# Cross-attention over 32 batches: output adds ahead of a transposition, and the sum of the attention output kept in PSUM

## The chip, the cores and the metric

The kernel runs on one core of a Trainium2 chip. The metric is the device time of one launch in microseconds; the time before is the median of three runs.

Engines are named as in the profile: PE is TensorE (PEld its weight loads), DVE is VectorE, ACT is ScalarE, POOL is GpSimd, SP is SyncE, which here only issues DMAs.

## The reference, cut to what matters

The inputs are `x` (32, 512, 640) and a context (32, 77, 1024), all in float32. The context's first 77 rows are the text keys, and there are only 77, so the object, other and image-prompt parts of the reference are empty and add nothing. What is left:

```
q = heads(x @ to_q_w)                  # 20 heads of 32
k = heads(ctx @ to_k_w); v = heads(ctx @ to_v_w)
p = softmax(q @ k.T / sqrt(32))        # over 77 keys
out = merge(p @ v) @ to_out_w + to_out_b + x
```

## The kernel before, in words

**Precision.** Every float32 operand of a matrix product is split into a high part, rounded to the fast float32 format of PE, and a low part, the rest. A product is then three matmuls: high by high, high by low, low by high. So each operand costs one cast on ACT (the high part) and one subtraction on DVE or POOL (the low part).

**Stages.** The first part of the program (about 300 us) makes keys and values for all batches and leaves them in DRAM. Then come 160 *slots*: slot n is batch b = n // 5 and a group of four heads j = n % 5. `slot` (line 661) writes out by hand, in program order, what each engine's queue holds; there is no scheduler behind it (`manual_schedule`), and every engine works its own queue in order. Semaphores between engines follow from which tiles the instructions touch.

**One slot.** On PE it holds, in this order: the scores of the first 128 queries (`scores(n, 0)`, three matmuls, line 453); six matmuls of the next slot's query projection (`queries`, line 434, tile `pq`); scores 1; nine more `pq` matmuls; scores 2; a piece of the output projection (`piece`, line 604, matmuls of line 589 into tile `po`); the product of probabilities and values (`values`, six matmuls of line 545 into tile `pa`); scores 3; a second `piece`.

On DVE a slot holds the row maxima of each score tile (line 461, `nm`); the low part of the probabilities (line 524, `pp`); the reciprocal of the sums (481); the low part of the attention output (571, `at`); the transposition of the probabilities (493, `z`); the low part of the next queries (104, `qt`); two adds that form the attention output (558); the adds that close output tiles (618, `xr`); and in some slots the transposition of the next batch's `x` (255).

ACT does the exponentials (471) and the casts (`qt` 103, `pp` 517 and 523, `at` 566, `xt` 262) and copies half of `pa` out of PSUM (556). POOL normalizes the probabilities (486), makes the last low part (531) and adds the bias to the residual (582).

**A lag.** The probabilities of slot n go through a transposition and through DRAM (`transpose_p`, `load_p`), and come back three slots later: in slot n the `values` are those of slot n - 3. The output projection of batch b - 1 starts when its five head groups are there, at j = 2 of batch b, in ten pieces over five slots (`STEPS`, `CUTS`, `PIECES`).

**The fourth slot, j = 3.** Its first piece (piece 2, six matmuls) multiplies the fifth head group into the two halves of the first 128 output rows and closes both. Its second piece (piece 3, 18 matmuls) opens the next output tiles. There are only two `po` buffers, so piece 3 can start only when the adds of line 618, called by `finish`, have read the two closed tiles. Before the change these adds stand on DVE's queue behind the `z` transposition and the `qt` subtraction of the slot.

**The sum of the attention output.** `values` leaves four partial results in `pa`, a PSUM tile of two banks with a single buffer. `sum_a` copies the upper 64 partitions to an SBUF tile `aw` on ACT and adds the halves on DVE into `aw`, also in SBUF. `high_a` and `low_a`, which run early in the next slot, make the parts of `at` from `aw`:

```
nc.vector.tensor_tensor(aw[64 * p : 64 * p + 64, 0], pa[:64, p], aw[:64, p], ALU.add)   # sum_a
nc.scalar.copy(at[:, 0, :], aws[n][:, 0])                                               # high_a
nc.vector.tensor_tensor(at[:, 1, :], aws.pop(n)[:, 0], at[:, 0, :].bitcast(F32), ...)   # low_a
```

**The end.** `end` (line 763) runs the last three `take` calls (values, sum, high part, low part one after the other) among what is left of the output projection, and uses `pa`'s two banks for the last two output tiles (`begin(6, ...)` and `begin(7, ...)`).

Of the kernel before, what the change touches and what calls it, by code (L numbers as in the profile page):

```python
# [8 lines left out]
F32 = mybir.dt.float32  # L9
FPR = mybir.dt.float32r  # L10
AF = mybir.ActivationFunctionType
ALU = mybir.AluOpType
# [11 lines left out]
P = 128  # L24
# [27 lines left out]
def kernel(  # L52
# [25 lines left out]
    nc = tc.nc  # L78
    B, S, C = x.shape
# [307 lines left out]
    psv = tc.alloc_tile_pool(name="psv", bufs=3, space=PSUM, side="right", reuse_waits="tile")  # L387
    late = []

    raws, pps, ats, pds, sms, pqs, pas, aws, xrs, pos = ({} for _ in range(10))  # L390

    bias = main.tile([P, C], F32, name="bias")
    nc.sync.dma_start(bias, bo.unsqueeze(0).to_broadcast([P, C]))
# [53 lines left out]
    def scores(n, t):  # L447
        b, j = divmod(n, NC_)
        g = GROUP_OF[j]
        qt, kb = qts[n % 2], kbs[g]  # L450
        sc = ps.tile([P, S], F32, tag="sc", name="sc", bufs=3)
        for m, (a, c) in enumerate(PAIRS):
            nc.tensor.matmul(  # L453
                sc[:, :KCOLS],
                qt[:, a, t * P : (t + 1) * P],
                kb[:, j - GROUPS[g][0], c],
                start=(m == 0),
                stop=(m == 2),
            )
        nm = main.tile([P, HPC], F32, tag="nm", name="nm", bufs=3)  # L460
        nc.vector.tensor_reduce(  # L461
            nm, sc[:, :KCOLS].rearrange("p (h k) -> p h k", k=NKEY), AX.X, ALU.max, negate=True
        )
        return sc, nm
# [14 lines left out]
    def sums(n):  # L479
        rs = main.tile([P, NQ * HPC], F32, tag="rs", name="rs", bufs=2)  # L480
        nc.vector.reciprocal(rs, sms.pop(n))  # L481
        return rs
# [30 lines left out]
    def cast_p(n):  # L513

        raw = raws[n]
        pp = late[0].tile([P, 5, S], FPR, tag="pp", name="pp", bufs=1)
        nc.scalar.copy(pp[:, 0:2, :], raw[:, 0:2, :])  # L517
        pps[n] = pp

    def rest_p(n):  # L520

        raw, pp = raws[n], pps[n]
        nc.scalar.copy(pp[:64, 4, :], raw[:64, 2, :])  # L523
        nc.vector.tensor_tensor(  # L524
            pp[:, 2:4, :], raw[:, 0:2, :], pp[:, 0:2, :].bitcast(F32), ALU.subtract
        )
# [24 lines left out]
            )  # L551

    def sum_a(n):
        pa = pas.pop(n)
        aw = late[0].tile([P, 2, S], F32, tag="aw", name="aw", bufs=1)
        nc.scalar.copy(aw[:64], pa[64:])  # L556
        for p in range(2):
            nc.vector.tensor_tensor(aw[64 * p : 64 * p + 64, 0], pa[:64, p], aw[:64, p], ALU.add)  # L558
        aws[n] = aw

    def high_a(n):
        if n >= N - NC_ + 1:
            at = xpool[0].tile([P, 2, S], FPR, tag="xt", name="at", bufs=7)
        else:
            at = late[0].tile([P, 2, S], FPR, tag="at", name="at", bufs=8)
        nc.scalar.copy(at[:, 0, :], aws[n][:, 0])  # L566
        ats[n] = at

    def low_a(n):
        at = ats[n]  # L570
        nc.vector.tensor_tensor(  # L571
            at[:, 1, :], aws.pop(n)[:, 0], at[:, 0, :].bitcast(F32), ALU.subtract
        )

    def load_residual(b, t, xr=None):
# [8 lines left out]
    def output_bank(b, t, h):  # L584
        pos[b, t, h] = late[1].tile([P, S], F32, tag="po", name="po", bufs=2)

    def project(b, t, h, j):
        for m, (a, c) in enumerate(PAIRS):
            nc.tensor.matmul(  # L589
                pos[b, t, h][:, :HALF],  # L590
                ats[b * NC_ + j][:, a, t * P : (t + 1) * P],
                wos[0][:, j, c, h * HALF : (h + 1) * HALF],
                start=(j == 0 and m == 0),
                stop=(j == NC_ - 1 and m == 2),
            )
# [8 lines left out]
    def piece(b, i):  # L604
        for t, h, j in STEPS[CUTS[i] : CUTS[i + 1]]:
            if j == 0:
                output_bank(b, t, h)
            project(b, t, h, j)
            if j == NC_ - 1:
                closed.append((b, t, h))  # L610

    def finish():

        while closed:
            b, t, h = closed.pop(0)
            xr = xrs[b, t]
            cols = slice(h * HALF, (h + 1) * HALF)
            nc.vector.tensor_tensor(  # L618
                xr[:, cols], pos.pop((b, t, h))[:, :HALF], xr[:, cols], ALU.add
            )  # L620
            if (b, t) == (B - 1, NQ - 1):
                nc.sync.dma_start(out[b, t * P : (t + 1) * P, cols], xr[:, cols])
            elif h == 1:
                nc.sync.dma_start(out[b, t * P : (t + 1) * P, :], xr)
# [23 lines left out]
    def refill(b, j, part):  # L648

        heads = range(2 * part, 2 * part + 2)  # L650
        segments = SEGMENTS[4 * part : 4 * part + 4]
        if j == 0:
            load_keys(b, 1, heads)
        elif j == 1:
            load_values(b, 0, segments)
        elif j == 2 and b + 1 < B:
            load_keys(b + 1, 0, heads)
        elif j == 3:
            load_values(b, 1, segments)

    def slot(n, beside=()):
        b, j = divmod(n, NC_)
        ahead, more = n + 1 < N, b + 1 < B
        back, first = PIECES[j]
        bo_, has_out = b - back, b >= back
        xsplits = SPLIT_X.get(j, ((), ())) if more and n > LATE else ((), ())
        turns = TRANSPOSE_X.get(j, ((), (), ())) if more and b else ((), (), ())
        if b == 1 and j < 2:
            turns = (((), (), ()), ((0, 1), (2,), ()))[j]
        taken = takes.get(n)  # L670

        filling = taken is not None and not has_out
        if not filling:
            refill(b, j, 0)
        if taken is not None:
            cast_p(taken)
        if n - 1 in takes:
            high_a(takes[n - 1])
        s = scores(n, 0)
        if taken is not None:  # L680
            rest_p(taken)
        rs = sums(n - 1) if n else None
        if taken is not None:
            last_p(taken)
        if n:
            normalize(n - 1, rs)
        if n - 1 in takes:
            low_a(takes[n - 1])
        exps(n, 0, *s)
        if ahead:  # L690
            queries(n + 1, 0, 2)
        s = scores(n, 1)
        if n - LAG + 1 in pds and n > LATE:
            load_p(n - LAG + 1)
        if filling:
            refill(b, j, 0)
        if n == NC_:
            load_x(b + 1, (2, 3))
        for k in WO.get(n, ()):
            nc.sync.dma_start(wos[0][:, k].bitcast(F32), wo_dram[:, k].bitcast(F32))  # L700
        refill(b, j, 1)
        finish()
        if j == 4 and b and b + 2 < B:
            load_x(b + 2, (0, 1))
        if j in RESIDUAL and b >= RESIDUAL[j][0]:
            load_residual(b - RESIDUAL[j][0], RESIDUAL[j][1])
        if j in BIAS and b >= BIAS[j][0]:
            add_bias(b - BIAS[j][0], BIAS[j][1])
        exps(n, 1, *s)
        for i in turns[0]:  # L710
            transpose_x(b + 1, i)
        if ahead:
            queries(n + 1, 2, NC_)
        s = scores(n, 2)
        if not ahead:
            exps(n, 2, *s)
            piece(bo_, first)
            s = scores(n, 3)
        if n and has_out:
            transpose_p(n - 1)  # L720
        if ahead:
            split_q(n + 1)
            exps(n, 2, *s)
        if n and not has_out:
            transpose_p(n - 1)
        if j == 4 and b + 2 < B:
            load_x(b + 2, (0, 1) if not b else (2, 3))
        for c in xsplits[0]:
            split_x(b + 1, c)
        if not ahead:  # L730
            exps(n, 3, *s)
            finish()
            piece(bo_, first + 1)
            take(taken)
            return
        if has_out:
            piece(bo_, first)
        else:
            s = scores(n, 3)
        if taken is not None:  # L740
            values(taken)
        if len(beside) > 0:
            context_values(LAST, beside[0], psv)
        if j == 3:
            finish()
        if has_out:
            s = scores(n, 3)
        finish()
        for i in turns[1]:
            transpose_x(b + 1, i)  # L750
        if taken is not None:
            sum_a(taken)
        for c in xsplits[1]:
            split_x(b + 1, c)
        exps(n, 3, *s)
        if len(beside) > 1:
            context_values(LAST, beside[1], psv)
        if has_out:
            piece(bo_, first + 1)
        for i in turns[2]:  # L760
            transpose_x(b + 1, i)
# [96 lines left out]
    for n in range(LATE, N):  # L858
        slot(n)
# [41 lines left out]
```

## Time and profile before

| | |
|---|---|
| median of 3 runs | 2065.09 us (2062.93 to 2071.85) |
| the profiled execution | 2066.77 us, span 2065.0 us |
| PE | 1956.2 us busy, 95% of the span |
| PEld | 1737.1 us, 84% |
| DVE | 1581.4 us, 77% |
| ACT | 1540.4 us, 75% |
| POOL | 1057.4 us, 51% |
| mean granted clock of PE | 0.975 |
| HBM traffic | 208 GB/s over the span |

Matmuls are pipelined and their ends are modelled, so PE's busy time is not time at its peak. The shares are means over the first part, in which DVE and ACT work at some 40%, and the slots, in which they work at over 80%. The order of work repeats every five slots, once for each batch, so the timeline of one batch stands for nearly all.

### The profile page before, as it was taken

The numbers are of one execution on the slowest core, as the hardware profiler recorded it, in microseconds if no ns is written. First come the engines' busy times: TensorE is split into PE (matmuls) and PEld (weight loads), VectorE is DVE, ScalarE is ACT, GpSimd is POOL, SyncE is SP. The second block draws the span as 40 slices with busy tenths as digits, with TensorE's granted clock in tenths as the row PEclk, the third lists the DMA queues.
The fourth block names the chain that finished last, engine by engine and source line by source line (L and its number), as shares of the span: only waits on it lengthen the run. The fifth ranks groups of instructions, "written<-read, shape, count | busy, mean of one in ns | idle before, by whom it ended". The sixth has DMA issues, their size and how long they took to land.

```text
span 2065.0 us, 36489 instructions
## 1 busy us (share of the span) xinstructions
PE 1956.2 (95%) x10332; PEld 1737.1 (84%) x10332; DVE 1581.4 (77%) x2334; ACT 1540.4 (75%) x6210; POOL 1057.4 (51%) x648
## 2 busy tenths in 40 slices
PE   9999997999999999999999999999999999999997
PEld 7787886888888888888888888888888888888886
DVE  4444447888888888888888888888888888888884
ACT  3232248888888888888888888888888888888882
POOL 1000125555665565565555555555665565556543
PEclk9999998999999999999999999999999999999999
DMA  9878787888888888888888888888888888888874
GB/s 184 203 178 233 180 200 206 233 207 219 219 206 212 223 213 208 214 214 213 210 219 214 214 220 211 214 215 210 222 204 213 223 213 212 212 214 213 213 191 134
DMA packets 568281, 431.29 MB, mean 209 GB/s; under 512 B 195344, under 2 KB 477072, under 8 KB 568080
## 3 DMA queue, kind: packets, MB, share of 16 engines
q1 hardware_dynamic: 564848, 417.65, 80.4%
q0 software_dynamic: 3136, 11.14, 1.5%
q8 instruction: 84, 1.38, 0.3%
q14 instruction: 117, 0.96, 0.1%
q10 hardware_dynamic: 96, 0.16, 0.0%
HBM read 247.17 MB, written 181.64 MB: 208 GB/s over the span
## 4 chain that ended last, share of the span: by engine, by line
PE 40%; ACT 16%; issue 15%; DVE 13%; POOL 11%; DMA 3%; SPq 1%; POOLq 0%; DVEq 0%; ACTq 0%
PE po L589 15%; PE pq L434 11%; POOL pn L486 8%; ACT pn L471 6%; PE sc L453 5%; PE pa L545 5%; ACT aw L556 3%; POOL pp L531 3%; PE pv L191 2%; PE pk L191 2%; DVE at L571 2%; DVE aw L558 2%; DMA pd<-z 2%; DVE qt L104 2%; ACT pp L523 2%
## 5 line engine op out<-in xcount | busy, mean ns | idle before, releaser
L471 ACT ACTIVATE pn<-sc,nm 128x77 f32<-128x77 f32 x2560 | 800.6, 333 | 221.5 <-DVE nm L461 217.4
L589 PE MATMUL po<-wo_s,at 128*128 128x320 f32 x3840 | 667.5, 323 | 81.6 <-DVE xr L618 65.3
L589 PEld LDWEIGHTS po<-wo_s,at 128*128 128x128 f32 x3840 | 606.8, 198 | 106.7 <-DVE xr L618 85.1
L434 PE MATMUL pq<-xt,wq_s 128*128 128x512 f32 x2400 | 607.3, 394 | 0.0
L531 POOL TENSOR_TENSOR pp<-raw,pp 64x512 fp32r<-64x512 f32 x160 | 217.5, 1360 | 662.4 <-ACT pp L523 589.4
L471 ACT ACTIVATION_READ_ACCUMULATOR pn<-sc,nm 128x1 f32 x2560 | 542.9, 212 | 0.0
L434 PEld LDWEIGHTS pq<-xt,wq_s 128*128 128x128 f32 x2400 | 438.1, 189 | 75.6
L486 POOL TENSOR_TENSOR pn<-pn,rs 128x1232 f32<-128x1232 f32 x160 | 412.8, 2580 | 59.7 <-DVE rs L481 48.9
L453 PE MATMUL sc<-kb,qt 128*128 128x308 f32 x1920 | 379.6, 306 | 11.8 <-ACT pn L471 8.5
L461 DVE TENSOR_REDUCE nm<-sc 128x4 f32<-128x308 f32 x640 | 296.0, 467 | 111.8 <-PE sc L453 107.3
L453 PEld LDWEIGHTS sc<-kb,qt 128*128 128x128 f32 x1920 | 326.6, 189 | 57.5 <-ACT pn L471 9.5
L493 DVE STREAM_TRANSPOSE z<-pn 128x1280 f32<-128x1280 f32 x160 | 241.8, 1511 | 115.6 <-POOL pn L486 100.4
L545 PE MATMUL pa<-pp,vb 128*128 128x512 f32 x960 | 253.3, 399 | 1.6 <-DVE pp L524 0.8
L524 DVE TENSOR_TENSOR pp<-raw,pp 128x1024 fp32r<-128x1024 f32 x160 | 208.1, 1301 | 45.6 <-ACT pp L517 44.4
L558 DVE TENSOR_TENSOR aw<-pa,aw 64x512 f32<-64x512 f32 x320 | 216.0, 675 | 33.9 <-ACT aw L556 27.9
L571 DVE TENSOR_TENSOR at<-aw,at 128x512 fp32r<-128x512 f32 x160 | 236.0, 1475 | 3.0 <-ACT at L566 3.0
L263 POOL TENSOR_TENSOR xt<-xs,xt 128x512 fp32r<-128x512 f32 x160 | 203.2, 1290 | 65.1 <-ACT xt L262 34.7
L556 ACT COPY aw<-pa 64x1024 f32<-64x1024 f32 x160 | 161.7, 1011 | 72.4 <-PE pa L545 70.9
L545 PEld LDWEIGHTS pa<-pp,vb 128*128 128x128 f32 x960 | 175.3, 189 | 32.2 <-DVE pp L524 1.1
L582 POOL TENSOR_TENSOR xr<-xr,bias 128x640 f32<-128x640 f32 x128 | 200.0, 1564 | 0.1
L517 ACT CAST pp<-raw 128x1024 fp32r<-128x1024 f32 x160 | 168.9, 1055 | 4.4 <-DMA raw<-pd 4.4
L191 PE MATMUL pk<-ct,wk_s 128*128 128x512 f32 (+1 forms) x600 | 139.3, 392 | 8.4 <-ACT ct L103 5.9
(42 smaller groups left out, 1364.7 us busy)
## 6 DMA issues: line engine op xcount, KB each, us to landing
pd<-z SPq DMA_DIRECT2D x640, 160.0 KB, 3.1
raw<-pd SPq DMA_DIRECT2D x160, 512.0 KB, 3.9
xs<-in_x_dram SPq DMA_DIRECT2D x128, 320.0 KB, 5.7
xr<-in_x_dram SPq DMA_DIRECT2D x128, 320.0 KB, 3.7
out_dram<-xr SPq DMA_DIRECT2D x127, 320.0 KB, 3.9
raw<-pd SPq DMA_DIRECT2D x160, 128.0 KB, 4.1
v_dram<-vs SPq DMA_DIRECT2D x80, 192.0 KB, 4.0
k_dram<-ks POOLq DMA_DIRECT2D x20, 512.0 KB, 3.3
```

Of the source, the lines that this page charges most:

```text
L434: nc.tensor.matmul(pqs[n], wq_s[:, k, a, j * P : (j + 1) * P], xts[b, k][:, c, :], start=(k == 0 and m == 0), stop=(k == NC_ - 1 and m == 2),)
L453: nc.tensor.matmul(sc[:, :KCOLS], qt[:, a, t * P : (t + 1) * P], kb[:, j - GROUPS[g][0], c], start=(m == 0), stop=(m == 2),)
L461: nc.vector.tensor_reduce(nm, sc[:, :KCOLS].rearrange("p (h k) -> p h k", k=NKEY), AX.X, ALU.max, negate=True)
L471: nc.scalar.activation(pnb[n % 2][:, at, :NKEY], sc[:, i * NKEY : (i + 1) * NKEY], AF.Exp, bias=nm[:, i : i + 1], accum_out=sms[n][:, at : ...
L486: nc.gpsimd.tensor_tensor(pf, pf, rs.unsqueeze(2).to_broadcast([P, NQ * HPC, NKEY]), ALU.mult)
L493: nc.vector.transpose(z.rearrange("p b t j -> p t b j"), pn.rearrange("p (t h) k -> p t (h k)", t=NQ).rearrange("p t (b i) -> p t b i", i=Q),)
L531: nc.gpsimd.tensor_tensor(pp[64:, 4, :], raw[:64, 2, :], pp[:64, 4, :].bitcast(F32), ALU.subtract)
L545: nc.tensor.matmul(pas[n][:, p, :], vb[:, p, t, :], pp[:, c, :], start=(c == p), stop=(t == 1),)
L556: nc.scalar.copy(aw[:64], pa[64:])
L558: nc.vector.tensor_tensor(aw[64 * p : 64 * p + 64, 0], pa[:64, p], aw[:64, p], ALU.add)
L571: nc.vector.tensor_tensor(at[:, 1, :], aws.pop(n)[:, 0], at[:, 0, :].bitcast(F32), ALU.subtract)
L589: nc.tensor.matmul(pos[b, t, h][:, :HALF], ats[b * NC_ + j][:, a, t * P : (t + 1) * P], wos[0][:, j, c, h * HALF : (h + 1) * HALF], start= ...
```

## The change

There are two edits.

In slot j = 3 the first piece and the call of `finish` that closes its two outputs move ahead of `transpose_p` and `split_q`. On PE nothing moves: the matmuls stand in the same order as before. On DVE the two adds of line 618 now stand ahead of the `z` transposition and the `qt` subtraction. On SP's queue the store of the finished output rows stands ahead of the four stores of `z`. ACT and POOL keep their order.

In `sum_a` the two adds of DVE write their result back into `pa` in PSUM, and `aw` keeps only the copied half (64 partitions). `high_a` and `low_a` read `pa`. In the built program the second of the two adds now also waits on a semaphore of DVE itself, which it did not before. `pa` is released by `low_a`, in the next slot, and no longer by the adds.

```diff
     def sum_a(n):
-        pa = pas.pop(n)
-        aw = late[0].tile([P, 2, S], F32, tag="aw", name="aw", bufs=1)
-        nc.scalar.copy(aw[:64], pa[64:])
+        pa = pas[n]
+        aw = late[0].tile([64, 2, S], F32, tag="aw", name="aw", bufs=1)
+        nc.scalar.copy(aw, pa[64:])
         for p in range(2):
-            nc.vector.tensor_tensor(aw[64 * p : 64 * p + 64, 0], pa[:64, p], aw[:64, p], ALU.add)
-        aws[n] = aw
+            nc.vector.tensor_tensor(pa[64 * p : 64 * p + 64, 0], pa[:64, p], aw[:, p], ALU.add)
 
     def high_a(n):
...
-        nc.scalar.copy(at[:, 0, :], aws[n][:, 0])
+        nc.scalar.copy(at[:, 0, :], pas[n][:, 0])
         ats[n] = at
 
     def low_a(n):
         at = ats[n]
         nc.vector.tensor_tensor(
-            at[:, 1, :], aws.pop(n)[:, 0], at[:, 0, :].bitcast(F32), ALU.subtract
+            at[:, 1, :], pas.pop(n)[:, 0], at[:, 0, :].bitcast(F32), ALU.subtract
         )
...
             piece(bo_, first)
             s = scores(n, 3)
+        if j == 3 and has_out:
+            piece(bo_, first)
+            finish()
         if n and has_out:
             transpose_p(n - 1)
         if ahead:
...
         if has_out:
-            piece(bo_, first)
+            if j != 3:
+                piece(bo_, first)
         else:
             s = scores(n, 3)
         if taken is not None:
             values(taken)
         if len(beside) > 0:
             context_values(LAST, beside[0], psv)
-        if j == 3:
-            finish()
         if has_out:
             s = scores(n, 3)
         finish()
```

## The prediction

> **What bounds the kernel now.** I read the page first. PE is the bound by its busy share (95%); DVE and ACT are at 77 and 75% of a span whose first 15% uses them less than half, so in the slots they are near 84% (the page's slices, and a mean of 167 to 168 us busy in the 200 us windows from 400 to 2000 us). Next I asked which wait PE still has:
>
> ```profile
> PE 1956.2 (95%) x10332; PEld 1737.1 (84%) x10332; DVE 1581.4 (77%) x2334; ACT 1540.4 (75%) x6210; POOL 1057.4 (51%) x648
> L589 PE MATMUL po<-wo_s,at 128*128 128x320 f32 x3840 | 667.5, 323 | 81.6 <-DVE xr L618 65.3
> PE po L589 <- DVE xr L618: 65.3, 33, 3.4
> PE po L589 <- DVE at L571: 8.6, 30, 0.9
> ```
>
> The group's row says that 81.6 us of PE's 109 us of idle time stand before one kind of matmul; the list of waits says whom it waited for: 33 times the closing adds, 2 us each, and 30 times the low part of `at`. One batch has one of each, so I looked at the fourth slot in the timeline (start, duration, engine, instruction, idle time before):
>
> ```profile
> 1018.93 1.67 DVE L571 TENSOR_TENSOR at<-aw,at 128x512 fp32r<-128x512 f32 x1
> 1019.52 0.59 PE L453 MATMUL sc<-kb,qt 128*128 128x308 f32 x3
> 1020.13 2.60 POOL L486 TENSOR_TENSOR pn<-pn,rs 128x1232 f32<-128x1232 f32 x1
> 1020.52 0.85 DVE L461 TENSOR_REDUCE nm<-sc 128x4 f32<-128x308 f32 x2
> 1020.65 0.85 PE L589 MATMUL po<-wo_s,at 128*128 128x320 f32 x4 [0.25 <-DVE at L571]
> 1021.34 1.55 PE L545 MATMUL pa<-pp,vb 128*128 128x512 f32 x6
> 1022.74 0.58 PE L453 MATMUL sc<-kb,qt 128*128 128x308 f32 x3
> 1022.77 1.51 DVE L493 STREAM_TRANSPOSE z<-pn 128x1280 f32<-128x1280 f32 x1 [1.39 <-POOL pn L486]
> 1024.20 0.65 DVE L104 TENSOR_TENSOR qt<-pq,qt 128x512 fp32r<-128x512 f32 x1
> 1024.78 0.87 DVE L618 TENSOR_TENSOR xr<-po,xr 128x320 f32<-128x320 f32 x2
> 1025.31 2.91 PE L589 MATMUL po<-wo_s,at 128*128 128x320 f32 x18 [1.99 <-DVE xr L618]
> ```
>
> The two `po` tiles are complete at about 1021.4, but DVE first idles 1.39 us for POOL, transposes, makes `qt`, and only then closes them. PE stands still from 1023.3 to 1025.31. Everything else on PE in this batch follows without a gap.
>
> The stall costs a second time. In the next batch the same 18 matmuls take 4.42 us instead of 2.91, and the windows' row shows the granted clock there:
>
> ```profile
> 1078.87 4.42 PE L589 MATMUL po<-wo_s,at 128*128 128x320 f32 x18 [1.99 <-DVE xr L618]
> 1078.80:1082.20 3.40, 3.33 (x15) 3.33 (x16) 2.17 (x5) 3.37 (x11) 3.17 (x3) 0.64 0.95 201
> ```
>
> The clock is 0.64 over this stretch, and 0.50 in each full microsecond of its middle. It was 1.00 in the same stretch of the batch before. Of the 31 such stalls in the timeline 20 are followed by the long form, 11 by the short, and from the first of them to the last the granted clock is halved nowhere else.
>
> **The change part by part.** *The adds ahead of the transposition.* They need the six matmuls of piece 2 (end about 1021.4, or 0.4 earlier without the wait for `at`) and two row maxima ahead of them. Two adds take 0.87 us, so they end by about 1022.3, before PE reaches the 18 matmuls at 1023.3. Of the waits 30 are of about 1.98 us (65.3 less the last three, 1.47, 1.16 and 3.35, leaves 59.3) and one, in the last batch, is of 1.47; these 31 go: 60.8 us. The 1.16 and the 3.35 lie elsewhere in the last batch and stay.
>
> What is moved back: DVE's `z` and `qt` now stand behind a wait for PE and 0.87 us of adds. The cover is that DVE idles 1.39 us there anyway, for POOL's normalization, which ends at 1022.73. `z` so starts when it did, `qt` ends at about 1024.85 as now, and the fourth row maximum comes 0.87 us earlier. Who waits for `qt` is scores 0 of the next slot; PE, no longer stopped, gets there at 1023.3 + 18 x 0.146 = 1025.9. So the next thing that could be late has about 1 us to spare; without that cover each late microsecond would stop PE in every batch. On SP the store of the output rows now stands ahead of the four `z` stores; it issues in 0.72 us and waits for adds that end before `z` does: nothing.
>
> *The slow clock.* If the 2 us stall goes, I take the half clock with it: 20 x (4.45 - 2.91) = 30.8 us. The row is my reason: no half clock follows the stalls of 0.25 us, nor the one of 1.47 us. The Trainium skill ("TensorE: Matmul & The Clock Gate", Part 1) speaks against this: it lets the clock fall after an idle window of about 3.4 us, and the idle time here is 2 us. By that rule the half clock would have another cause and stay, and the sum would be 30.8 us higher; the measured coincidence, 20 of 20, decides for me.
>
> *The sum in PSUM.* `low_a` has two SBUF inputs and takes 1.62 us in the median where POOL works beside it, but 0.69 at the end, where POOL is idle. Read from PSUM, its shape is that of the `qt` subtraction, 0.65 us. That is 160 x (1.475 - 0.654) = 131 us of DVE's time. On the path lies little of it: the 30 waits of PE for `at` go, 8.6 us; bounds are 0 and 12 (the four matmuls start 0.4 us late by their own rhythm). `high_a` reads PSUM at 0.60 instead of 0.63: nothing on the path.
>
> No row of this trace writes PSUM from DVE. The nearest is the add itself, 0.68 us with a PSUM input and SBUF output. In its new form I bound it by 0.64 us, its fastest now, and by 1.36, if a write to PSUM cost as much again, and take 0.68, since only the output moves; the new wait of the second add on the first is bounded by 0 and by a whole add, and I take 0.05, near the hop from ACT's copy to DVE's add in the tail (0.03). Both lie on DVE, which has just been given 0.95 us a slot, so nothing on the path.
>
> `pa` is held until `low_a`. In the fourth slot `low_a` ends 0.74 us before PE writes `pa` again, in the other four 1.8 us or more (1009.77 against 1011.61 in the third); with the shorter `low_a` these grow by 0.95. Nothing in the slots. In the tail it costs: the 12 matmuls of `begin(6)`, at 2053.81, wait for the adds, which end at 2053.66; now they wait for the low part, which ends at 2055.09. That is 1.4 us, once.
>
> **Sum.** 60.8 + 30.8 + 8.6 - 1.4 = 98.8 us. The profiled execution took 2066.77 us, 1.7 above the median; 2066.8 - 98.8 = 1968.0, or 1966 against the median. I predict 1967. A cross-check: batches are now 54.59 us apart on average (1583.13 us between 30 stalls); 53.57 - 1.98 - 0.3 = 51.3 us would be left, and ACT, 45.5 us busy in a batch, and DVE, 45.8 less 4, still fit into that.
>
> **Rivals.** *The half clock stays*, for the reason given or because a shorter gap still sets it off: 2066.8 - 68 = 1999 us. For it: the gap's limit is not known better than between 1.47 and 2 us. Chance 0.12.
>
> *The stall moves.* ACT and DVE, which PE now outruns, become late elsewhere: `qt` in the fourth slot, or the `xr` adds in the fifth and first, where the 12 matmuls at 1046.44 already take 2.31 us instead of 1.92. Against: ACT idles 1.2 us in each of these slots because of the slow `low_a`, which ends. If half of the stall returned, the half clock mostly gone, 2066.8 - 30 - 25 = 2012 us; if all of it returned, with the clock, about 2058, which is no change. Chance 0.12, of which 0.03 for the last.
>
> *Slower: `pa` is released too late.* `low_a` stands on DVE behind `pp`, which waits for ACT's cast. If it ended later than PE's next `values` by d, PE would stop d in all 155 slots. It decides against the change from d = 0.7 (155 x 0.7 = 108 us, more than the gain); that needs `low_a` to end 1.4 us later than now in the fourth slot and 2.5 in the others, while its own time shrinks. The dear end of the adds' price, 2 x 0.68 less the 0.95 saved, is 0.4 of these. At d = 0.8 the time is 2066.8 - 99 + 124 = 2092 us. Chance 0.04.
>
> *It does not do what it says*: only if the adds could not run early, for instance for the bias; but POOL adds it a slot ahead (line 582, ended by 1013.5). No chance of its own.
>
> **How the numbers follow.** Forecast 0.72, half clock stays 0.12, stall moves 0.12, slower 0.04. The forecast's own range: below, the 0.39 us still hidden in the first slot goes too (31 x 0.39 = 12, 1955); above, half of the half clocks stay and the wait for `at` too (1967 + 15 + 9 = 1991). To hold 8 in 10 it reaches to the first rival: 1952 to 2000. About 0.5%, 10 us, is what can be told from no change. Faster 0.93, same 0.03, slower 0.04.
>
> **What would show it.** Right: the wait of line 589 for `xr` falls from 33 to 2 or 3 and below 6 us, that for `at` disappears; the 18 matmuls take 2.7 to 2.9 us in every batch and the mean clock rises from 0.975 to about 0.99; the subtraction of `at` takes 0.65 us; batches lie 51.3 us apart. Wrong: matmuls of line 453 wait for `qt`, those of 545 for `at`, or half-clock stretches stand where no gap precedes them.

## The result, and the profile after

The changed kernel takes 1960.84 us (median of 4 runs, 1960.07 to 1961.89) against 2066.44 us before (here the median of 4): a ratio of 0.9487, 95% interval 0.9465 to 0.9509. A second series, with its own runs of the kernel before, gave 1959.99 us and 0.9478 (0.9465 to 0.9491). The profiled execution took 1961.89 us (span 1959.8, mean clock 0.992). The forecast was 1967, within 1952 to 2000.

From line 559 on a line of the changed kernel has a number one lower than before: the closing adds are 617, the projection 588, the low part of `at` 570.

From the page after: PE's busy share, the projection's group (busy time, mean ns, idle time before it and its releaser) and the normalization; then the waits that answer to the two shown before. The last two rows are those of the normalization and of the subtraction of `at` in the kernel before.

```profile
PE 1909.2 (97%) x10332; PEld 1704.8 (87%) x10332; DVE 1436.2 (73%) x2334; ACT 1534.3 (78%) x6210; POOL 1002.3 (51%) x648
L588 PE MATMUL po<-wo_s,at 128*128 128x320 f32 x3840 | 626.0, 311 | 21.5 <-DVE xr L617 14.2
L486 POOL TENSOR_TENSOR pn<-pn,rs 128x1232 f32<-128x1232 f32 x160 | 364.4, 2278 | 32.9 <-DVE rs L481 20.5
```

```profile
PE po L588 <- DVE xr L617: 14.2, 18, 3.0
PE po L588 <- DVE at L570: 4.4, 3, 4.0
```

```profile
L486 POOL TENSOR_TENSOR pn<-pn,rs 128x1232 f32<-128x1232 f32 x160 | 412.8, 2580 | 59.7 <-DVE rs L481 48.9
L571 DVE TENSOR_TENSOR at<-aw,at 128x512 fp32r<-128x512 f32 x160 | 236.0, 1475 | 3.0 <-ACT at L566 3.0
```

PE's idle time before the projection fell from 81.6 to 21.5 us. DVE is 145 us less busy; the subtraction of `at` takes 628 ns instead of 1475. POOL's normalization, which the change does not touch, went from 2580 to 2278 ns.

The fourth slot of one batch in the timeline after:

```profile
570.88 0.63 DVE L570 TENSOR_TENSOR at<-pa,at 128x512 fp32r<-128x512 f32 x1
571.81 0.59 PE L453 MATMUL sc<-kb,qt 128*128 128x308 f32 x3
572.02 2.28 POOL L486 TENSOR_TENSOR pn<-pn,rs 128x1232 f32<-128x1232 f32 x1
572.24 1.05 PE L588 MATMUL po<-wo_s,at 128*128 128x320 f32 x6
572.95 0.89 DVE L617 TENSOR_TENSOR xr<-po,xr 128x320 f32<-128x320 f32 x2
573.13 1.55 PE L545 MATMUL pa<-pp,vb 128*128 128x512 f32 x6
574.34 1.51 DVE L493 STREAM_TRANSPOSE z<-pn 128x1280 f32<-128x1280 f32 x1 [0.49 <-POOL pn L486]
574.52 0.58 PE L453 MATMUL sc<-kb,qt 128*128 128x308 f32 x3
574.94 2.80 PE L588 MATMUL po<-wo_s,at 128*128 128x320 f32 x18
575.77 0.65 DVE L104 TENSOR_TENSOR qt<-pq,qt 128x512 fp32r<-128x512 f32 x1
```

The adds run beside the `pa` matmuls, 0.5 us before `z` could start, and the 18 matmuls follow scores 3 with no gap. They take 2.80 us in all 31 fourth slots, never 4.4; over the slot shown the granted clock is 1.00. No half clock is left between the first and the last of these blocks.

**Where the time went.** The starts of the 18 matmuls divide each profile into a first part, 30 batches and a tail:

| us | before | after |
|---|---|---|
| up to the first block of 18 | 370.68 | 368.82 |
| 30 batches | 1635.67 | 1533.18 |
| tail | 58.64 | 57.80 |

Inside the 30 batches I added up how much later each matmul started after the one before it than its regular distance (146 ns behind a matmul of `po`, 232 behind one of `pq` or `pa`, 142 behind one of `sc`). This is called lateness below:

| us over 30 batches | forecast gain | before | after |
|---|---|---|---|
| ahead of the 18 matmuls (stall) | 60.8 | 63.6 | 0.0 |
| inside the 18 (half clock) | 30.8 | 33.5 | 0.2 |
| inside piece 2 (wait for `at`) | 8.6 | 14.1 | 0.25 |
| inside the second piece of the first slot (wait for `xr`) | 0 | 11.6 | 20.5 |

The four differences come to 102 of the 102.5 us. About 3 of the 33 us inside the 18 are not the clock: a block that starts after a stall takes 2.91 us at the full clock, one without a stall 2.80.

### The profile page after: what moved, and what is told of

It reads as the page before. It is cut to its first block, busy times and chain, and to the rows that moved or that the text cites. A ratio compares the mean times of both kernels' runs of the same rounds, so it can differ in the third digit from the quotient of the medians.

```text
span 1959.8 us, 36241 instructions
## 1 busy us (share of the span) xinstructions
PE 1909.2 (97%) x10332; PEld 1704.8 (87%) x10332; DVE 1436.2 (73%) x2334; ACT 1534.3 (78%) x6210; POOL 1002.3 (51%) x648
## 4 chain that ended last, share of the span: by engine, by line
PE 21%; DMA 19%; issue 17%; ACT 16%; DVE 12%; POOL 11%; SPq 3%; DVEq 0%; POOLq 0%; ACTq 0%
DMA raw<-pd 8%; ACT pn L471 8%; DMA pd<-z 8%; POOL pn L486 7%; PE pq L434 6%; PE po L588 6%; POOL pp L531 3%; DVE pp L524 3%; PE pv L191 3%; PE sc L453 2%; PE pk L191 2%; ACT xt L262 2%; ACT aw L556 2%; DVE nm L461 2%; DVE z L493 2%
## 5 line engine op out<-in xcount | busy, mean ns | idle before, releaser
L588 PE MATMUL po<-wo_s,at 128*128 128x320 f32 x3840 | 626.0, 311 | 21.5 <-DVE xr L617 14.2
L588 PEld LDWEIGHTS po<-wo_s,at 128*128 128x128 f32 x3840 | 576.6, 189 | 32.2 <-DVE xr L617 24.6
L531 POOL TENSOR_TENSOR pp<-raw,pp 64x512 fp32r<-64x512 f32 x160 | 211.1, 1319 | 663.6 <-ACT pp L523 390.4
L486 POOL TENSOR_TENSOR pn<-pn,rs 128x1232 f32<-128x1232 f32 x160 | 364.4, 2278 | 32.9 <-DVE rs L481 20.5
L524 DVE TENSOR_TENSOR pp<-raw,pp 128x1024 fp32r<-128x1024 f32 x160 | 195.5, 1222 | 91.8 <-ACT pp L517 86.7
L558 DVE TENSOR_TENSOR pa<-pa,aw 64x512 f32<-64x512 f32 x320 | 222.7, 696 | 31.5 <-ACT aw L556 22.2
L191 PEld LDWEIGHTS pk<-ct,wk_s 128*128 128x128 f32 x600 | 116.2, 195 | 30.8 <-ACT ct L103 7.2
```

The lines of the kernel that those rows point to most:

```text
L191: nc.tensor.matmul(held[j][:, :gn], w[:, k, a, :], cts[g, k][:, c, :gn], start=(k == 0 and n == 0), stop=(k == NK - 1 and n == 2),)
L486: nc.gpsimd.tensor_tensor(pf, pf, rs.unsqueeze(2).to_broadcast([P, NQ * HPC, NKEY]), ALU.mult)
L524: nc.vector.tensor_tensor(pp[:, 2:4, :], raw[:, 0:2, :], pp[:, 0:2, :].bitcast(F32), ALU.subtract)
L531: nc.gpsimd.tensor_tensor(pp[64:, 4, :], raw[:64, 2, :], pp[:64, 4, :].bitcast(F32), ALU.subtract)
L558: nc.vector.tensor_tensor(pa[64 * p : 64 * p + 64, 0], pa[:64, p], aw[:, p], ALU.add)
L588: nc.tensor.matmul(pos[b, t, h][:, :HALF], ats[b * NC_ + j][:, a, t * P : (t + 1) * P], wos[0][:, j, c, h * HALF : (h + 1) * HALF], start= ...
```

## The experiments

Each time is a median, with the ratio to the kernel before on the same chip.

**Each part alone.** The order alone keeps `sum_a`, `high_a` and `low_a` as before:

```diff
+        if j == 3 and has_out:
+            piece(bo_, first)
+            finish()
         if n and has_out:
             transpose_p(n - 1)
...
-        if j == 3:
-            finish()
```

> The order of the changed kernel with the sum of the attention output kept in SBUF, as before. Theory (the adds' place carries nearly all): the stall of 1.98 us in the fourth slot and the half clock after it are gone, the wait of piece 2 for the low part of at stays (0.4 us a batch, 13 to 14 us in all), and POOL's normalization stays at 2.60 us, so the wait for xr in the first slot of a batch stays or grows: 1975 to 1990 us, mean clock 0.99. Rival (the sum in PSUM is what shortens the way to the adds): no less than 2030 us, with the stall in the timeline.

Measured: 2018.54 us, ratio 0.9762 (0.9747 to 0.9776). Neither expectation held. The stall of the fourth slot and the half clock were gone, as the theory said, but the time was 28 us above its range. The list of waits and a first slot in the timeline:

```profile
PE po L589 <- DVE xr L618: 50.5, 32, 3.4
PE po L589 <- DVE at L571: 10.4, 30, 1.2
```

```profile
1075.64 1.66 DVE L571 TENSOR_TENSOR at<-aw,at 128x512 fp32r<-128x512 f32 x1
1076.83 2.61 POOL L486 TENSOR_TENSOR pn<-pn,rs 128x1232 f32<-128x1232 f32 x1
1077.73 0.33 ACT L471 ACTIVATE pn<-sc,nm 128x77 f32<-128x77 f32 x1 [1.17 <-DVE nm L461]
1079.47 1.51 DVE L493 STREAM_TRANSPOSE z<-pn 128x1280 f32<-128x1280 f32 x1 [1.40 <-POOL pn L486]
1081.87 0.47 DVE L618 TENSOR_TENSOR xr<-po,xr 128x320 f32<-128x320 f32 x1
1082.40 1.15 PE L589 MATMUL po<-wo_s,at 128*128 128x320 f32 x6 [1.56 <-DVE xr L618]
```

The stall moved two slots on, to the second piece of the first slot, whose add also stands behind POOL's normalization and the transposition. The lateness there grew from 11.6 to 54.3 us, and batches took 52.9 us. In this slot ACT idles 1.17 us for maxima that stand behind the slow subtraction, and DVE 1.40 us for the normalization: with PE's stop gone, the ring of ACT, DVE and POOL is late.

The sum in PSUM alone:

```diff
-        aw = late[0].tile([P, 2, S], F32, tag="aw", name="aw", bufs=1)
-        nc.scalar.copy(aw[:64], pa[64:])
+        aw = late[0].tile([64, 2, S], F32, tag="aw", name="aw", bufs=1)
+        nc.scalar.copy(aw, pa[64:])
...
-            nc.vector.tensor_tensor(aw[64 * p : 64 * p + 64, 0], pa[:64, p], aw[:64, p], ALU.add)
+            nc.vector.tensor_tensor(pa[64 * p : 64 * p + 64, 0], pa[:64, p], aw[:, p], ALU.add)
```

> The sum in PSUM alone, the closing adds behind the transposition as before. Theory: the subtraction of at takes 0.63 us and POOL's normalization 2.28, the wait for at goes (14 us), the stall before the 18 matmuls stays at 1.5 to 2 us in every batch. If the half clock needs an idle time of more than 1.5 us it comes in fewer batches: 2020 to 2052 us. Rival (the sum in PSUM carries the gain): below 1985 us.

Measured: 2010.80 us, ratio 0.9727 (0.9712 to 0.9741), 9 us below the theory's range. The stall stayed, but shorter, and no half clock followed it in the 30 batches:

```profile
999.41 2.91 PE L588 MATMUL po<-wo_s,at 128*128 128x320 f32 x18 [1.64 <-DVE xr L617]
```

Of the 56 us that the 30 batches gained, the clock made 30, the wait for `at` 14 and the shorter stall 10. So either part alone takes the half clock away, and each leaves a stall (53 or 54 us) that only both together remove.

**How long a gap the clock takes.** The sum in PSUM, with the adds between `z` and `qt`:

```diff
         if n and has_out:
             transpose_p(n - 1)
+        if j == 3 and has_out:
+            piece(bo_, first)
+            finish()
```

> The sum in PSUM, and the closing adds between the transposition z and the qt subtraction: a stall of 0.6 to 0.7 us less than with the adds behind both. Theory of the half clock (it follows an idle time of PE somewhere between 1.47 and 1.97 us): a stall of 0.8 to 1.4 us in every batch and no half clock in the slots, 1961 + 31 x 1.1 = 1995 us (1980 to 2006). Rival (any repeated gap of about 1 us sets it off): half clocks in two of three batches, 2020 us or more.

Measured: 1993.43 us, ratio 0.9641 (0.9626 to 0.9656), as the theory said. The blocks of 18 in its timeline:

```profile
995.26 2.91 PE L588 MATMUL po<-wo_s,at 128*128 128x320 f32 x18 [1.03 <-DVE xr L617]
1047.31 2.91 PE L588 MATMUL po<-wo_s,at 128*128 128x320 f32 x18 [1.03 <-DVE xr L617]
```

In the slots half clocks followed gaps of 1.96 us and more (before) and none of 1.03 (here), 1.56 (the order alone) or 1.64 us (PSUM alone).

Length alone does not decide, though: before the change only 20 of 31 nearly equal gaps were followed. The trace's records of the granted clock show what tells them apart. In each profile they change only at times that lie whole multiples of 3.41 us apart. The next rows, of PE in the kernel before, are two such stretches with a gap, each with the stretch behind it:

```profile
1021.76:1025.17 3.41, 1.56 (x8) 1.00 0.69 193
1025.17:1028.58 3.41, 3.28 (x22) 1.00 0.94 197
1076.37:1079.78 3.41, 1.42 (x10) 1.00 0.62 147
1079.78:1083.20 3.41, 3.41 (x15) 0.50 0.91 224
```

Both gaps are of 1.99 us. The first is cut by the end of its stretch into 1.85 and 0.14 us, and the clock stays at 1.00. The second lies whole in its stretch, and the next stretch runs at 0.50. So it is throughout: the 20 gaps that were followed each lie whole in one stretch, with 1.96 us or more; of the other 11, ten are cut, with 1.87 us at most in one stretch, and one is of 1.47.

**What the sum in PSUM pays for.** The order of the changed kernel, the sum in SBUF, and the low part at another place on DVE's queue:

```diff
         s = scores(n, 0)
+        if n - 1 in takes:
+            low_a(takes[n - 1])
         if taken is not None:
             rest_p(taken)
...
-        if n - 1 in takes:
-            low_a(takes[n - 1])
         exps(n, 0, *s)
```

> The order of the changed kernel with the sum in SBUF, as in the run of the order alone (2018.5 us), but with the low part of at moved on DVE's queue to before the low part of the probabilities, where POOL is idle. Theory (the sum in PSUM pays because a subtraction with two SBUF inputs and POOL's work lock each other out, not because PSUM is read faster): the subtraction takes 0.65 to 0.70 us with both inputs in SBUF, POOL's normalization 2.28, and most of the 58 us between the order alone and both parts comes back: 1962 to 1985 us. Rival (it is the read from SBUF that is slow, or the longer chain of DVE in any place): the subtraction stays over 1 us, 2005 us or more.

Measured: 2068.61 us, ratio 1.0009 (0.9998 to 1.0019): the time is the rival's, the durations are the theory's. The groups' rows:

```profile
L531 POOL TENSOR_TENSOR pp<-raw,pp 64x512 fp32r<-64x512 f32 x160 | 366.0, 2288 | 605.9 <-ACT pp L523 502.8
L486 POOL TENSOR_TENSOR pn<-pn,rs 128x1232 f32<-128x1232 f32 x160 | 364.0, 2275 | 50.0 <-DVE rs L481 38.6
L571 DVE TENSOR_TENSOR at<-aw,at 128x512 fp32r<-128x512 f32 x160 | 110.7, 692 | 108.7 <-ACT at L566 108.7
```

With both inputs in SBUF the subtraction takes 0.69 us where POOL is idle, and the normalization 2.28. So SBUF is not slow to read; the 1.62 us were a wait for POOL. In the profile before, the 136 subtractions that met a running instruction of line 531 took 1.62 us on average, the other 24 took 0.63. Of the 136, 134 ended 0.55 us after that POOL instruction did. But the lockout only moved: now `pp` on DVE (line 524) meets line 531, which takes 2.29 us on average instead of 1.36 before, and DVE idles 109 us for ACT's high part first. That eats the whole gain of the order. What this run does not separate is how much of its time the new place costs without any lockout.

**The tail.**

```diff
-        for i in range(3, 6):
-            begin(i, 0, 4)
+        begin(3, 0, 4)
         take(N - 1)
+        for i in range(4, 6):
+            begin(i, 0, 4)
```

> The changed kernel with 24 matmuls of the last batch (begin(4) and begin(5)) moved on PE to behind the last values, so that PE has work while the last sum, high part and low part are made. Theory (holding pa until the low part costs 1.4 us in the tail, a wait of 3.96 us instead of 2.60, and this gap sets off a half clock that costs 1.6 us): the wait falls below 0.6 us, no half clock in the last 20 us: 1955.5 to 1958 us. Rival (the tail ends by the stores and closing adds): 1960 us or more.

Measured: 1952.99 us, ratio 0.9460 (0.9444 to 0.9476), below the range. The block after the last `values`, in the kernel before, in the changed kernel and then in this one:

```profile
2053.81 7.27 PE L589 MATMUL po<-wo_s,at 128*128 128x320 f32 x48 [2.60 <-DVE aw L558]
1947.03 8.85 PE L588 MATMUL po<-wo_s,at 128*128 128x320 f32 x48 [3.96 <-DVE at L570]
```

```profile
1939.55 7.31 PE L588 MATMUL po<-wo_s,at 128*128 128x320 f32 x48 [0.45 <-DVE at L570]
```

The gap and the half clock in it are gone; the tail went from 57.8 to 54.2 us, as expected. The other 4 us are in batches that the edit does not touch (1527 us against 1533 and 1528 in two profiles of the changed kernel), so I do not count them as its gain.

**The wait that is left.** In the first slot the same move:

```diff
-        if j == 3 and has_out:
+        if j in (0, 3) and has_out:
...
-            if j != 3:
+            if j not in (0, 3):
```

> The changed kernel, with the same move in the first slot of a batch too (j = 0: the add that closes tile (2, 0) ahead of z and qt). Theory (what PE still waits for in a batch is this add, 20.5 us in all, because it stands behind the transposition): 1940 us (1936 to 1946), the wait for xr within the slots gone. Rival (that wait only shows that ACT, DVE and POOL are the bound now): no change, 1957 to 1965 us, with PE waiting elsewhere, for qt or for the maxima's tiles.

Measured: 1954.74 us, ratio 0.9451 (0.9435 to 0.9467): between the two. The lateness of 20.5 us in the first slot went, and 22 of 30 batches came to 50.4 to 50.7 us. But 11.9 us appeared one slot on, three times by 1.9 to 2.3 us at once, at an add that stands behind probabilities which came late from DRAM. Together with the tail edit:

> The moved add of the first slot together with the moved matmuls of the tail. Theory: the two gains add up, 1954.7 - 4 = 1951 us (1948 to 1954). Rival (the tail change gives nothing): 1954 us or more.

Measured: 1946.16 us, ratio 0.9426 (0.9407 to 0.9445), 2 us below the range: the gains of the two moves at least add up.

Next, on the changed kernel, the loads of `x` spread over two slots, to have the probabilities back earlier:

```diff
-        if b == 1 and j < 2:
+        if b and j < 2 and more:
             turns = (((), (), ()), ((0, 1), (2,), ()))[j]
...
-        if n == NC_:
+        if j == 0 and b and more:
             load_x(b + 1, (2, 3))
...
-        if j == 4 and b and b + 2 < B:
-            load_x(b + 2, (0, 1))
...
-            load_x(b + 2, (0, 1) if not b else (2, 3))
+            load_x(b + 2, (0, 1))
```

> The changed kernel with the second half of the next x loaded in the first slot of a batch instead of the fifth, and its first transposition in the second slot instead of the first, as the kernel does for one batch already. Theory (in the changed kernel some batches take 51.8 us instead of 50.75 because the probabilities come back late from DRAM while x is loaded: ACT waited 43 us for raw, 31 times): the wait for raw falls under 15 us, batches come to 50.7 to 50.9 us, 1950 to 1957 us. Rival (not the DMA but the adds in the first slot make the difference, and DVE has more to do in the second slot): 1959 to 1975 us.

Measured: 1966.75 us, ratio 0.9521 (0.9507 to 0.9535). The time lies in the rival's range. But ACT's wait for `raw` hardly moved (43.0 to 39.4 us), the first slot's lateness stayed at 20.4 and the 30 batches took 1535 us: the edit did not do what it was for, so it does not tell whether late probabilities make the batches differ.

And closing adds put earlier in the next slot, on top of the moved add and the tail:

```diff
         s = scores(n, 0)
+        finish()
         if taken is not None:
             rest_p(taken)
```

> The moved add of the first slot, the moved matmuls of the tail (together 1946.2 us), and the adds that close the second piece of each slot put ahead of the low part of the probabilities in the next slot, instead of behind the second row maximum. Theory (what PE still waits for, 7 us at the first piece of the second slot, is this add, kept back by probabilities that come late from DRAM): that wait goes, 1938 to 1944 us. Rival (the late probabilities stop PE at the next place instead): 1945 to 1950 us.

Measured: 1953.55 us, ratio 0.9453 (0.9440 to 0.9466), 7 us more than without and above both ranges: the wait for the add went, and waits of PE's scores (about 8 us) took its place, as the rival has it.

The first piece's adds ahead of the transposition in all slots, on the changed kernel:

```diff
-        if j == 3 and has_out:
+        if ahead and has_out:
             piece(bo_, first)
             finish()
...
-            if j != 3:
-                piece(bo_, first)
+            pass
```

> The changed kernel with the first piece's adds ahead of the transposition in all five slots. In the second, third and fifth slot DVE then waits for the 12 matmuls of the piece, up to 1.75 us after the third scores, before it transposes. Theory (DVE has slack there, and the adds that matter are those of the first slot): like the run with the first slot's add alone, 1950 to 1957 us. Rival (a DVE that stands waiting for PE makes the transposition, its stores and the late probabilities later): 1960 us or more.

Measured: 1944.43 us, ratio 0.9408 (0.9387 to 0.9429), with runs from 1939.92 to 1952.06; better than the theory's range. That DVE waits for 12 matmuls in the other slots does no harm that shows. The second series of the changed kernel was on the same chip:

> The changed kernel once more, on the chip of the two runs that follow: 1958 to 1963 us. Its batches differ by up to 1 us from one another (50.75 to 51.84 us), so the 30 batches together may differ by 5 us from the first profile.

Measured: 1959.99 us (1956.64 to 1962.07). Last, all slots together with the tail edit:

> The first piece's adds ahead of the transposition in all five slots (1944.4 us alone) and the moved matmuls of the tail (the tail, from the last 18 matmuls of a fourth slot to the end, 54.3 us instead of 57.9). Theory: 1944.4 - 3.6 = 1941 us (1936 to 1946). Rival (the run with all slots was a lucky one of a spread of 12 us, and only the first slot's add counts): as the first slot's add with the tail, 1946 to 1951 us.

Measured: 1941.78 us, ratio 0.9390 (0.9374 to 0.9405). That is the lowest time of all versions, 19 us under the changed kernel's 1960.84.

## Why the prediction was right, and where not

**The stall: right, for an incomplete reason.** The place of the adds does remove the 2 us. But I wrote that what is moved back has cover because "DVE idles 1.39 us there anyway", and that behind it the next late thing has 1 us to spare. The order alone shows what that misses: the chain then bounds the kernel in the first slot, 54 us of lateness. The rival "the stall moves", at 2012 us, is what the order alone does, at 2018.5, and in a place that the rival named. Even in the changed kernel one sign failed: I expected 2 or 3 waits of the projection for `xr`, below 6 us in all, and it has 18, of 14.2 us.

**The step that failed is the size of the sum in PSUM.** I gave it 8.6 us with "On the path lies little of it". Taken away from the changed kernel it costs 2018.5 - 1960.8 = 58 us, of which 55 are in the 30 batches. There the lateness shows where: 34 us in the first slot (54.3 instead of 20.5) and 15 at the wait for `at` (15.6 instead of 0.25). The wait for `at` I had too small because I took PE's displayed idle time, 0.29 us a batch, where the matmuls started 0.4 us late and more. The 34 us I had priced at nothing. They come from two savings: the subtraction gets 1 us shorter (1608 ns with the order alone, 628 in the changed kernel), and POOL's normalization 0.3 us, which I left out. Its fastest row, 2270 ns against a median of 2603, stood in the profile before. In the timeline of the order alone both stand on the way, the first ahead of ACT, the second ahead of DVE; how the 34 us divide between them no run shows.

The Trainium skill ("SBUF — State Buffer", Who interferes with whom) says that a DVE instruction with two SBUF inputs and a GpSimd instruction that reads SBUF share a read port and block one another; the run with the moved low part agrees, 0.69 against 1.62 us on DVE and 2.28 against 2.60 on POOL.

The total came out within 6 us because I counted the whole stall to the order and took for granted the slack that the sum in PSUM gives: the total was right, the division was not. The rival "the stall moves" does name that slack (ACT's idle time "because of the slow `low_a`, which ends"), but the sum has no price for it. Some of the closeness is luck: stall, half clock and wait for `at` were together about 10 us larger than forecast, and the first slot's lateness, put at nothing, grew by 9.

**The half clock: right.** It went, and it was worth the forecast 30 us (33 less the 3 of slower starts). The prediction sets a rule of the Trainium skill against it ("TensorE: Matmul & The Clock Gate", Part 1: an idle window of about 3.4 us). The records show stretches of that length, 3.41 us, but one need not be idle throughout: 1.96 us in one of them was enough before the change, and 1.87 was not. With the moved low part, where the gaps are of 2.3 us, 14 of 30 were followed: those with 1.91 us or more in one stretch, while the other 16 had at most that. So why 20 of 31, which looked like chance, is where each gap fell.

The limit is not one number, and I misjudged it: "between 1.47 and 2 us" leaves out a gap of 1.46 us in the tail of the kernel before, at 2040.54, behind which the clock was halved too. The same gap, of 1.45 to 1.48 us, was followed in 11 of the 14 profiles, and one of 1.76 in a slot with the first slot's add moved. What more than the idle time of a stretch counts there stays open.

**PSUM's prices: right.** The adds take 696 instead of 675 ns each, the pair 1.43 instead of 1.37 us with its new wait; nothing on the path.

**The tail: right.** The wait before the last 48 matmuls went from 2.60 to 3.96 us, 1.4 as forecast. That it also drew a half clock there (8.85 instead of 7.27 us) I had not foreseen; another in the tail, in a block of 46 matmuls, fell away (8.54 us in the kernel before, 7.00 now).

**Missed.** Batches now differ, 50.74 to 51.84 us, though no half clock falls among them. ACT's wait for probabilities from DRAM came up:

```profile
ACT pp L517 <- DMA raw<-pd: 43.0, 31, 3.7
pd<-z SPq DMA_DIRECT2D x640, 160.0 KB, 3.9
```

ACT's wait was 4.4 us before, and the stores of `z` then landed in 3.1 us. That these late probabilities make the batches differ is suggested by the chain of waits, but the one attempt to change it moved nothing, so it stays open.

## What to carry to other kernels

Where PE waits for a short closing step, look at what stands ahead of that step on its engine's queue, not at the step: moving it can cost nothing if it reads data that is long there. But count the whole ring of engines that turns with it: with PE's stop gone, the next chain is right behind, and a saving that looks off the path (here, that DVE and POOL no longer lock each other out) may be what decides whether the gain is half or whole. And look at the clock after each repeated gap: here 30 of the 102 us gained in the batches were the half clock that a 2 us gap brought with it.

## What the runs showed of the hardware that I had not expected

A DVE subtraction with two SBUF inputs and POOL's work did not share but excluded each other: 1.62 us instead of 0.63, ending 0.55 us after POOL's instruction in 134 of 136 cases, and in the moved form 2.29 us on POOL instead of 1.36.

The half clock came in stretches of 3.41 us that start at fixed distances. In the slots before the change it followed a stretch with 1.96 us of idle PE and not one with 1.87, so that equal gaps of 1.99 us were followed or not by where they fell. In the tail 1.46 us could be enough.
